# Convolution and attention on one core: vectors laid out by products, a first norm by blocks, and biases in another order

## The chip, the cores and the metric

The kernel runs on 1 core of a Trainium2 chip. Its time is device time in microseconds (us). The kernel before took 2860.66 us, the median of 6 runs (2857.87 to 2861.8). The profile is that of one more execution. Engines: PE multiplies matrices (and is fed by weight loads), DVE is the vector engine, ACT the scalar engine, POOL the general one, SP issues DMAs.

## The reference

For 4 images of 384 channels and 48x48 pixels (N = 2304 tokens) it computes a block of a network:

```python
local = lax.conv_general_dilated(x, conv_w, window_strides=(1, 1), padding='SAME', ..., feature_group_count=C)   # 7x7, each channel alone
inv = bn_gamma * lax.rsqrt(bn_var + BN_EPS)
local = local * inv[None, :, None, None] + (bn_beta - bn_mean * inv)[None, :, None, None]
x_norm = _layernorm(x_flat, ln_gamma, ln_beta)
qkv = x_norm @ qkv_w.T + qkv_b            # 8 heads of 48
q = q + _layernorm(local_flat, ln_gamma, ln_beta)   # by heads
attn = jax.nn.softmax(jnp.einsum('bhnd,bhmd->bhnm', q, k) * scale, axis=-1)
out = jnp.einsum('bhnm,bhmd->bhnd', attn, v)
return x_flat + (out @ proj_w.T + proj_b)
```

All is float32.

## The kernel before

**Tiles.** Channels lie on the 128 partitions in three chunks, in an order packed by heads (`segments`): each load of a group is four DMAs. Tokens come in groups of 384 (8 image rows), 6 groups to an image, 24 groups (`t`) in all. A group of three blocks of 128 tokens is the unit of the norms, of the queries and of the convolution; its convolution reads a slab of up to 14 rows (8 and 3 on each side).

**Norm.** The class `Norm` (L355 to L468) does a layer norm over channels: the mean by a product with a matrix of 1/384 on PE (`mean`, L386, or `mean_of`, through `project`, L473), centring on DVE (L401), squares on ACT (L364), the mean of the squares, Ln, Exp and a square on ACT (`root`, L406 to L408), two Newton steps on DVE (L413, L414) and the scaling (L468). Norms of later groups sum the three chunks on DVE (L374, L375) and send one product to PE.

**Convolution.** `conv_ops` (from L229) yields one DVE instruction for each chunk and tap: 147 of them (3 x 49) for a group (L251 the first tap, L255 the others). All 24 groups form one stream, and `convolve_first(n)` or `convolve(point)` take the next n of it. Chunk 0 of the first group is special: its first `PE_TAPS` = 10 taps are made on PE, as products with diagonal matrices (`make_diagonals` on ACT, L263; `first_products`, L274), and are added by `add_products` (L825). `AHEAD` = 4 of chunk 0's other taps come first.

**Order.** The order of work on PE, DVE, ACT, SP and POOL is that in which the code is written, engine by engine; every engine takes its instructions in order. A planner (`plan`) spreads what is left of the stream over the half-slots of the attention, so that a group's steps are done when its norm is due.

**Head.** Batch-norm and layer-norm vectors and the taps are combined into `natural` (L160 to L165) and moved by 14 small DMAs (L175, on ACT's and POOL's queues) into `vec`, packed by heads. x of the first group and the slab of the first convolution are loaded apart (`load_x`, `load_slab`, L106), then three weight tensors (`staged`), then x of the other groups, and `w_o`. 12 warm-up products (`warm`, L830) run on PE, then the mean of the first group, 12 more, and the rest of the first norm. ACT scales the weights by the norm's gain (L605 for values, L612 and L613 for keys and queries). The beta part of the biases is made by `shift_rows` (L568, one row each on PE), `rows_out` (L580, L583, ACT) and `columns` (L594, PE), and added by `key_bias` and `query_bias` (L616 to L622, DVE).

**Keys and values.** `from_x` makes values (by blocks), keys and queries of a group, two products of the list at a time; each call of `both(making)` goes on by one pair. For the first image this is done group by group (the loop over g from 1 to 5), interleaved with the norm of the next group's x and with convolution steps; in the last round the norm is that of the first convolution (`local_end`, L642), and `query_end` (L651) adds it to the queries.

**Attention.** For each group t come 12 slots of two halves, each of three blocks of keys: `score` (L765 on PE, Exp on ACT, L773) and `weigh` (L786 on PE). After each pair of heads ACT copies and DVE adds the sums (L672, L681). In slots 8 and 10 of the first group, 6 and 9 of the others, the norm of the next group's convolution is done: sums on DVE, from t = 1 on with two small DMAs (`out`, `few_in`), `few_centre` on DVE (L445), squares as `jobs` between the Exps on ACT (L369). In slot 3 of t = 0 `output_bias` folds the value bias into the output bias: 9 products of one column, a copy on ACT (L634), an addition on DVE (L635).

**End.** The last six groups are projected; between them `judge` counts reciprocals outside a safe range: a comparison on DVE (L1071), a product on PE (L1073), a decision (L1076, L1077), a read.

Of the kernel before, what the change touches and what calls it, by code (L numbers as in the profile page):

```python
# [15 lines left out]
P = 128  # L16
NH = 8
HD = 48
# [8 lines left out]
X_LATER = 3  # L27
OUT_SLOT = 4
LAG = 2
AHEAD = 4  # L30
WARM = 12
PE_TAPS = 10

# [11 lines left out]
def unshifted_pass(  # L47
# [49 lines left out]
    def two_banks():  # L97
        return next(either)()

    def over_chunks(a):  # L100
        return a.rearrange("p (o g) -> p o g", o=1).to_broadcast([P, CC, G])

    def load_packed(dst, src, queue=nc.sync, tails=None):
        for p0, piece in segments(src):
            by = tails if tails and p0 % 64 else queue
            by.dma_start(out=dst[p0 : p0 + piece.shape[0]], in_=piece)  # L106


    xn = {}

    def load_x(b, g):
        t = big.tile([P, CC, G], F32, tag=f"xn{g}", name=f"xn{b}_{g}")
        load_packed(t, x[b, :, g * G : (g + 1) * G])
        xn[b, g] = t

    slabs = {}

    def load_slab(b, g, tails=None):
        first, end = max(0, g * RG - PAD), min(H, (g + 1) * RG + PAD)
        t = work.tile([P, CC, (RG + 2 * PAD) * W], F32, tag="slab", name=f"slab{b}_{g}")  # L120
        load_packed(t[:, :, 0 : (end - first) * W], x[b, :, first * W : end * W], tails=tails)
        slabs[b, g] = (t, first, end)


# [28 lines left out]
    nc.scalar.dma_start(out=norms[:, 4:6], in_=ln)  # L153
    taps_in = big.tile([P, CC, T0], F32, tag="kt0", name="taps_in")
    nc.scalar.dma_start(out=taps_in, in_=conv_w)
    load_x(0, 0)
    load_slab(0, 0)
    nc.gpsimd.tensor_scalar_add(inv, norms[:, 3], BN_EPS)
    nc.gpsimd.tensor_tensor(inv, inv, neg_half, ALU.pow)
    nc.vector.tensor_copy(natural[:, :, T0 + 1 :], norms[:, 4:6].rearrange("p v c -> p c v"))  # L160
    nc.vector.tensor_mul(inv, inv, norms[:, 0])
    nc.vector.tensor_mul(natural[:, :, T0], norms[:, 2], inv)
    nc.vector.tensor_sub(natural[:, :, T0], norms[:, 1], natural[:, :, T0])
    for c in range(CC):
        nc.vector.tensor_scalar(  # L165
            natural[:, c, 0:T0], taps_in[:, c], inv[:, c : c + 1], None, ALU.mult
        )
    queues = cycle((nc.gpsimd, nc.scalar, nc.gpsimd))
    for c in range(CC):
        for r, n, first in ((0, HD, 0), (64, HD, 1), (48, 16, 6), (112, 16, 7)):  # L170
            head = first + 2 * c if first < 6 else first
            ch = head * HD + (16 * c if first >= 6 else 0)
            while n:
                part = min(n, P - ch % P)
                next(queues).dma_start(  # L175
                    out=vec[r : r + part, c, :],
                    in_=natural[ch % P : ch % P + part, ch // P, :],
                )
                r, n, ch = r + part, n - part, ch + part

# [47 lines left out]
    def conv_ops(t):  # L230
        b, g = divmod(t, NG)
        if t + 1 < NT:
            load_slab(*divmod(t + 1, NG))
        slab, first, end = slabs[b, g]
        acc = work.tile([P, CC, G], F32, tag="acc", name=f"acc{t}", bufs=3)
        accs[t] = acc
        if t == 0:
            nc.vector.memset(acc[:, 0, :], 0.0)

        order = [(tap, c) for tap in taps for c in range(CC)]  # L240
        if t == 0:
            mine = [(tap, 0) for tap in taps[PE_TAPS:]]
            order = mine[:AHEAD] + [o for o in order if o[1]] + mine[AHEAD:]
        for tap, c in order:
            part = window(slab, acc[:, c, :], g, first, end, c, tap)
            if not part:
                continue
            src, dst = part
            weight = cw[:, c, tap : tap + 1]
            if tap == taps[0]:  # L250
                nc.vector.tensor_scalar(  # L251
                    dst, src, weight, shift[:, c : c + 1], ALU.mult, ALU.add
                )
            else:
                nc.vector.scalar_tensor_tensor(dst, src, weight, dst, ALU.mult, ALU.add)  # L255
            yield
# [93 lines left out]
    class Norm:  # L350
# [9 lines left out]
            self.src = src  # L360
            self.buf = work.tile([P, CC, G], F32, tag="sq", name="sq")

        def squares(self):
            nc.scalar.activation(self.buf, self.src, AF.Square)  # L364

        def square_jobs(self):

# [13 lines left out]
            self.add(self.buf)  # L381


        def mean(self):
            self.m = two_banks()[:, 0, :G]
            nc.tensor.matmul(self.m, lhsT=mean_w, rhs=self.buf[:, 0, :], start=True, stop=True)  # L386

        def mean_kept(self):
# [3 lines left out]
            self.m = self.buf[:, 0, :]  # L392
            nc.scalar.copy(self.m, m)

        def mean_of(self, src):

            self.m = two_banks()[:, 0, :G]
            project(self.m, lambda c: mean_w, lambda c: src[:, c, :])

        def centre(self):  # L400
            nc.vector.tensor_sub(self.src, self.src, over_chunks(self.m))  # L401

        def root(self):

            y, u = self.buf[:, 1, :], self.buf[:, 2, :]
            nc.scalar.activation(u, self.m, AF.Ln, bias=eps)  # L406
            nc.scalar.activation(y, u, AF.Exp, scale=-0.5)
            nc.scalar.activation(u, y, AF.Square, scale=0.5**0.5)  # L408

        def newton(self):  # L410

            y, u = self.buf[:, 1, :], self.buf[:, 2, :]
            nc.vector.scalar_tensor_tensor(u, self.m, eps, u, ALU.add, ALU.mult)  # L413
            nc.vector.scalar_tensor_tensor(y, u, -1.5, y, ALU.add, ALU.mult)  # L414
            return over_chunks(y)

# [47 lines left out]
            nc.vector.transpose(self.buf[:, 2, :], spread(y))  # L464
            return over_chunks(self.buf[:, 2, :])

        def scale(self, rs):
            nc.vector.scalar_tensor_tensor(self.src, self.src, -1.0, rs, ALU.mult, ALU.mult)  # L468


    def project(dst, weights, src, n=G):
# [77 lines left out]
    def both(making):  # L549
        next(making)  # L550
        next(making)
# [36 lines left out]
    def columns():  # L588

        r, r2 = two_banks(), two_banks()  # L590
        m = {1: r[:, 0, 0:CC], 2: r[:, 1, 0:CC], 0: r2[:, 0, 0:CC]}
        for i in m:
            for c in range(CC):
                nc.tensor.matmul(  # L594
                    m[i][:, c : c + 1],
                    lhsT=row[of_row(i), c * P : (c + 1) * P],
                    rhs=one[of_row(i)],
                    start=True,
                    stop=True,
                )  # L600
        return m

    def scale_values():
        for c in range(CC):
# [225 lines left out]
            nc.tensor.matmul(first_sum[:, 0:P], lhsT=mean_w, rhs=ident, start=True, stop=True)  # L830

    warm(WARM)
    norm = Norm(xn[0, 0])
    norm.mean_of(norm.src)
    warm(WARM)
    norm.centre()
    norm.squares()
    make_diagonals(0, 5)
    convolve_first(AHEAD)
    norm.mean_of(norm.buf)  # L840
    norm.root()
    scale_values()
    first_products(5)
    norm.scale(norm.newton())
    make_diagonals(5, PE_TAPS)
    for c in range(CC):
        scale_rows(1, c)

# [1 line left out]
    both(making)  # L850
    shift_rows()
    rows_out()
    first_products(PE_TAPS - 5)
    m = columns()
    convolve_first(14)
    norm = Norm(xn[0, 1])
    norm.sum()
    norm.mean()
    add_products()
    key_bias(m)  # L860
    query_bias(m)
    both(making)
    convolve_first(3)
    norm.centre()
    norm.squares()
    convolve_first(4)
    norm.sum_squares()
    norm.mean()
    norm.root()
    for c in range(CC):  # L870
        scale_rows(0, c)
    both(making)
    convolve_first(10)
    norm.scale(norm.newton())
    both(making)
    both(making)
    for g in range(1, NG):

        last = g == NG - 1
        making = from_x(0, g)  # L880
        both(making)
        convolve_first(4)
        assert not last or n_first >= each - PE_TAPS
        norm = Norm(accs[0] if last else xn[0, g + 1])
        norm.sum()
        norm.mean()
        convolve_first(6)
        norm.centre()
        norm.squares()
        both(making)  # L890
        convolve_first(3)
        norm.sum_squares()
        norm.mean()
        norm.root()
        both(making)
        convolve_first(8 if last else 12)
        if last:
            local_end(0, norm.newton())
        else:
            norm.scale(norm.newton())  # L900
        both(making)
        both(making)
# [3 lines left out]
    for t in range(NT):  # L906
# [52 lines left out]
        for s in range(NSLOT):  # L959
# [31 lines left out]
            if t and following and s == second:  # L991
                norm.few_variance()
            convolve("slot", t, s, 0)
            if t == 0 and s == CC:
                output_bias()
            if t == 0 and s in (first, second):
                norm.mean_kept()
            attend(t, s, 1)
# [37 lines left out]
    for before in range(NT - NG, NT):  # L1036
        ao = aos[before % NG]
        if before == NT - NG + 3:
            judge[0](two_banks()[:, 0, :])
        r, r2 = two_banks(), two_banks()  # L1040
        parts = r[:, 0, :G], r[:, 1, :G], r2[:, 0, :G]
        for co, m in enumerate(parts):
# [2 lines left out]
            finish(before, co, m, nc.scalar)  # L1045
        if before == NT - NG:
            rb = divide(NT - 1)
        if before == NT - NG + 3:
            judge[1]()
        if before == NT - NG + 2:  # L1050
            nc.vector.tensor_mul(outputs[NT - 1][0], outputs[NT - 1][0], rb)
        if before == NT - 2:
            n_outside = judge[2]()
    return n_outside


def conv_attention(tc: tile.TileContext, *args):
    nc = tc.nc
    few = NH * RG * 48 // P
    with tc.tile_pool(name="keep", bufs=1) as keep:  # L1060
# [6 lines left out]
        nc.vector.memset(inside, 1.0)  # L1067
        nc.vector.memset(ones, 1.0)

        def count(m):  # L1070
            nc.vector.tensor_scalar(outside, inside, 0.5, None, ALU.is_lt)  # L1071
            counts.append(m[0:1, :few])
            nc.tensor.matmul(counts[0], lhsT=ones, rhs=outside, start=True, stop=True)  # L1073

# [4 lines left out]
        def read():  # L1079
            return nc.values_load(flag[0:1, 0:1])  # L1080

        n_outside = unshifted_pass(tc, *args, inside, (count, decide, read))
        with tc.If(n_outside > 0):
            shifted_pass(tc, *args)

# [504 lines left out]
```

## Time and profile before

| What | Value |
| --- | --- |
| median of 6 runs | 2860.66 us |
| the profiled execution: whole time | 2859.14 us |
| its span, first to last instruction | 2857.4 us |
| PE busy | 2833.8 us (99%) |
| DVE busy | 2341.7 us (82%) |
| ACT busy | 1648.1 us (58%) |
| POOL busy | 17.3 us (1%) |
| DMA moved | 124.38 MB, mean 44 GB/s |
| mean granted clock of PE | 0.999 |

Times in the text are microseconds from the start of this span. In a timeline a line has start, length, engine, line of the code, operation, tile written, tiles read, and in brackets the idle time before it and what ended it. A float32 product shows as two records. The list of waits has who waited, for whom, the sum, the number and the longest. The chain of waits goes back from the last instruction to what released it.

### The profile page before, as it was taken

How to read it: one execution, taken by the hardware profiler on the slowest of the kernel's cores; microseconds unless marked ns; L12 is line 12 of the kernel's file. 1: busy time of each engine (PE TensorE's matmuls, PEld its weight loads, DVE VectorE, ACT ScalarE, POOL GpSimd, SP SyncE). 2: the span in 40 equal slices, each digit the busy share in tenths (PEclk: the TensorE clock that was granted, in tenths of full speed). 3: DMA queues.
4: the chain of work that ended last, by engine and by line, in shares of the span. 5: the costliest groups of instructions: out<-in, count | busy, mean ns of one | idle time of the engine just before them, and what ended most of it. 6: DMA issues, size and time to landing. Idle time of an engine off the chain costs nothing.

```text
span 2857.4 us, 70279 instructions
## 1 busy us (share of the span) xinstructions
PE 2833.8 (99%) x29540; PEld 1453.8 (51%) x29540; DVE 2341.7 (82%) x4613; ACT 1648.1 (58%) x2341; POOL 17.3 (1%) x82
## 2 busy tenths in 40 slices
PE   8999999999999999999999999999999999999998
PEld 5544444444554455555555445555555545555554
DVE  7999999999888888888888889888788887787301
ACT  4366666666226666666623666666642466666662
POOL 2000000000000000000000000000000000000000
PEclk9999999999999999999999999999999999999999
DMA  6101121101221111111132112102113110111111
GB/s 116 39 11 31 46 48 35 38 25 42 74 80 30 40 35 42 30 39 24 38 95 69 27 30 51 35 22 45 38 32 94 45 22 28 43 30 30 45 34 63
DMA packets 103689, 124.38 MB, mean 44 GB/s; under 512 B 43344, under 2 KB 89024, under 8 KB 103360
## 3 DMA queue, kind: packets, MB, share of 16 engines
q1 hardware_dynamic: 99568, 116.07, 16.9%
q8 instruction: 234, 3.83, 0.6%
q10 hardware_dynamic: 3088, 3.65, 0.4%
q14 instruction: 95, 0.78, 0.1%
q0 software_dynamic: 704, 0.06, 0.0%
HBM read 81.98 MB, written 27.03 MB: 38 GB/s over the span
## 4 chain that ended last, share of the span: by engine, by line
PE 95%; DVE 3%; DMA 1%; ACT 0%; issue 0%; ACTq 0%; SPq 0%; DVEq 0%
PE r L765 38%; PE o L786 38%; PE o L473 10%; PE r L473 9%; DVE acc L255 2%; DMA xn<-in_x_dram 1%; ACT pt L773 0%; DMA vec<-natural 0%; PE r L386 0%; DMA staged<-in_qkv_wT_dram 0%; DMA taps_in<-in_conv_w_dram 0%; PE o L386 0%; DVE sq L375 0%; DMA parts<-part 0%; DVE sq L374 0%
## 5 line engine op out<-in xcount | busy, mean ns | idle before, releaser
L773 ACT ACTIVATE pt<-r 128x768 f32<-128x768 f32 x1728 | 1399.0, 810 | 757.4 <-PE r L765 741.2
L255 DVE SCALAR_TENSOR_TENSOR acc<-slab,vec,acc 128x368 f32<-128x368 f32 (+6 forms) x3447 | 1756.8, 584 | 3.7 <-DMA qk_vec<-in_qk_b_dram 2.6
L786 PE MATMUL o<-pt,v 64*64 64x384 f32 x13824 | 1438.9, 482 | 0.0
L765 PE MATMUL r<-xn,k 48*64 48x384 f32 x10368 | 1080.6, 482 | 4.7 <-ACT pt L773 4.7
L786 PEld LDWEIGHTS o<-pt,v 64*64 64x64 f32 x13824 | 552.3, 132 | 566.2 <-issue 562.6
L765 PEld LDWEIGHTS r<-xn,k 48*64 48x64 f32 x10368 | 414.5, 132 | 430.7 <-issue 394.5
L765 PE MATMUL r<-qt,kt 48*64 48x384 f32 x3456 | 359.4, 481 | 0.1
L765 PEld LDWEIGHTS r<-qt,kt 48*64 48x64 f32 x3456 | 136.9, 132 | 143.1 <-issue 133.7
L681 DVE TENSOR_TENSOR ao<-o,ao 113x384 f32<-113x384 f32 x72 | 40.0, 555 | 193.3 <-PE r L765 176.3
L473 PE MATMUL o<-xn,w_qk 128*128 128x384 f32 x432 | 147.2, 486 | 0.0
L473 PE MATMUL r<-xn,w_qk 128*128 128x384 f32 x432 | 147.2, 486 | 0.0
L473 PEld LDWEIGHTS r<-xn,w_qk 128*128 128x128 f32 x432 | 82.1, 190 | 57.2
L473 PEld LDWEIGHTS o<-xn,w_qk 128*128 128x128 f32 x432 | 82.0, 190 | 57.4 <-ACT w_qk L613 0.4
L506 ACT COPY v<-r 128x384 f32<-128x384 f32 x43 | 18.6, 482 | 135.2 <-PE r L473 135.2
L473 PE MATMUL r<-w_v,xn 128*128 128x384 f32 x258 | 87.3, 487 | 0.0
L681 DVE TENSOR_TENSOR aot<-o,aot 113x384 f32<-113x384 f32 x24 | 13.3, 556 | 82.1 <-ACT aot L672 64.5
L473 PE MATMUL o<-af,w_o 128*128 128x384 f32 x222 | 75.0, 486 | 0.0
L374 DVE TENSOR_TENSOR sq<-sq 128x384 f32<-128x384 f32 x47 | 26.1, 554 | 58.4 <-ACT sq L369 56.5
L473 PEld LDWEIGHTS r<-w_v,xn 128*128 128x128 f32 x258 | 48.8, 190 | 35.2 <-issue 1.8
L473 PE MATMUL o<-w_v,xn 128*128 128x384 f32 x174 | 60.3, 486 | 1.5 <-DVE xn L468 1.5
L741 DVE SCALAR_TENSOR_TENSOR xr<-r,pb,xr 128x384 f32<-128x384 f32 x27 | 16.4, 617 | 52.4 <-ACT xn L525 42.4
L473 PEld LDWEIGHTS o<-af,w_o 128*128 128x128 f32 x222 | 42.1, 190 | 29.2
(128 smaller groups left out, 1030.4 us busy)
## 6 DMA issues: line engine op xcount, KB each, us to landing
xr<-in_x_dram SPq DMA_DIRECT2D x24, 576.0 KB
slab<-in_x_dram SPq DMA_DIRECT2D x32, 378.0 KB
held<-ao SPq DMA_DIRECT2D x20, 576.0 KB
af<-held SPq DMA_DIRECT2D x20, 576.0 KB
xn<-in_x_dram SPq DMA_DIRECT2D x48, 216.0 KB
rb<-rden SPq DMA_DIRECT2D x48, 216.0 KB
out_dram<-xr SPq DMA_DIRECT2D x54, 192.0 KB
slab<-in_x_dram SPq DMA_DIRECT2D x16, 297.0 KB
```

Source lines behind the costliest of these rows:

```text
L255: nc.vector.scalar_tensor_tensor(dst, src, weight, dst, ALU.mult, ALU.add)
L374: nc.vector.tensor_add(self.buf[:, 0, :], src[:, 0, :], src[:, 1, :])
L473: nc.tensor.matmul(dst, lhsT=weights(c), rhs=src(c), start=c == 0, stop=c == CC - 1)
L506: nc.scalar.copy(v[:, blk, :, 0:HD], r[:, :C].rearrange("p (h d) -> p h d", d=HD))
L681: nc.vector.tensor_add(dst, sums[0 : 64 + HA, 1, :G], dst)
L741: nc.vector.scalar_tensor_tensor(xr[:, co, :], m, pb[:, co : co + 1], xr[:, co, :], ALU.add, ALU.add)
L765: nc.tensor.matmul(r[h, j, :G], lhsT=kk[:, blk * P + h.start : blk * P + h.stop], rhs=qq, start=True, stop=True,)
L773: nc.scalar.activation(pt, r[:, :, :G], AF.Exp, scale=SCALE)
L786: nc.tensor.matmul(sums[halves[j], i, :G], lhsT=values[t // NG, kb // NB][h, first : first + 64], rhs=pt[h, j, :], start=kb == 0, stop=kb ...
```

## The change

- **Vectors.** The 14 DMAs into `vec` go. DVE fills `packing` with columns of the identity (a memset, 14 copies), and `pack` moves `natural` into `vec` with 7 products on PE and one copy on ACT.
- **Loads.** The first group's x is no longer loaded; the first slab comes in two parts, its 8 rows and then 3 rows of the next group, and the first norm reads the slab.
- **First norm.** Means, centring, squares, roots, Newton steps and scaling go by three blocks of 128 tokens; the second warm-up goes. `scale_values` stands between the second and the third root.
- **Convolution.** `PE_TAPS` becomes 8, 2 of them early; `AHEAD` goes: chunks 1 and 2 of the first group come first.
- **Biases.** The remaining diagonals, the scaling of the query weights and six products come behind the first keys; the mean of the next x comes right behind the columns, in a bank of theirs; the second pair of keys comes ahead of that norm's second mean.
- **Output bias.** `output_bias` moves from slot 3 of the first attention into the last round of keys, between 4 convolution steps and the sums of the local norm.
- **Judge.** The comparison is a function of its own, behind the last division.

```diff
-PE_TAPS = 10
+PE_TAPS = 8
+EARLY_TAPS = 2
...
-    load_x(0, 0)
-    load_slab(0, 0)
+    load_slab(0, 0, parts=2)
+    place_x(0, 0)
...
+    packing = big.tile([P, len(pairs), P], F32, tag="k1", name="packing")
+    nc.vector.memset(packing, 0.0)
+    for c, r, cc, r0, n in pieces:
+        nc.vector.tensor_copy(
+            packing[:, pairs.index((c, cc)), r : r + n], ident[:, r0 : r0 + n]
+        )
...
-                next(queues).dma_start(
-                    out=vec[r : r + part, c, :],
-                    in_=natural[ch % P : ch % P + part, ch // P, :],
+    def pack():
+        m = two_banks()[:, 0, 0 : CC * (T0 + 3)].rearrange("p (c v) -> p c v", c=CC)
...
+                nc.tensor.matmul(
+                    m[:, c, :],
+                    lhsT=packing[:, pairs.index(pair), :],
+                    rhs=natural[:, pair[1], :],
...
+        nc.scalar.copy(vec, m)
...
             mine = [(tap, 0) for tap in taps[PE_TAPS:]]
-            order = mine[:AHEAD] + [o for o in order if o[1]] + mine[AHEAD:]
+            order = [o for o in order if o[1]] + mine
...
     warm(WARM)
+    pack()
+
+    blocks = [slice(i * P, (i + 1) * P) for i in range(NB)]
+    raw = slabs[0, 0][0]
     norm = Norm(xn[0, 0])
-    norm.mean_of(norm.src)
-    warm(WARM)
-    norm.centre()
-    norm.squares()
-    make_diagonals(0, 5)
-    convolve_first(AHEAD)
-    norm.mean_of(norm.buf)
-    norm.root()
+    norm.mean_of(raw, blocks)
+    for at in blocks:
+        norm.centre(raw, at)
+        norm.squares(at)
+    convolve_first(2)
+    norm.mean_of(norm.buf, blocks)
+    norm.root(blocks[0])
+    make_diagonals(0, EARLY_TAPS)
+    norm.root(blocks[1])
     scale_values()
-    first_products(5)
-    norm.scale(norm.newton())
-    make_diagonals(5, PE_TAPS)
+    norm.root(blocks[2])
+    first_products(EARLY_TAPS)
+    for at in blocks:
+        norm.scale(norm.newton(at), at)
+        if at is blocks[1]:
+            convolve_first(3)
     for c in range(CC):
         scale_rows(1, c)
...
     rows_out()
-    first_products(PE_TAPS - 5)
-    m = columns()
-    convolve_first(14)
+    make_diagonals(EARLY_TAPS, PE_TAPS)
+    next(making)
+    for c in range(CC):
+        scale_rows(0, c)
+    first_products(PE_TAPS - EARLY_TAPS)
+    m, bank = columns()
+    convolve_first(10)
     norm = Norm(xn[0, 1])
     norm.sum()
-    norm.mean()
-    add_products()
+    norm.mean(bank)
+    convolve_first(7)
     key_bias(m)
     query_bias(m)
-    both(making)
-    convolve_first(3)
+    next(making)
     norm.centre()
     norm.squares()
-    convolve_first(4)
+    both(making)
+    add_products()
+    convolve_first(2)
     norm.sum_squares()
     norm.mean()
     norm.root()
-    for c in range(CC):
-        scale_rows(0, c)
     both(making)
-    convolve_first(10)
+    convolve_first(6)
     norm.scale(norm.newton())
     both(making)
-    both(making)
+    convolve_first(5)
...
         assert not last or n_first >= each - PE_TAPS
+        if last:
+            output_bias()
...
-            if t == 0 and s == CC:
-                output_bias()
...
         if before == NT - NG:
             rb = divide(NT - 1)
+            judge[0]()
```

## The prediction

> **What bounds the kernel now.** I read the page first, then PE's waits, then the chain of waits between 212 and 312 us, then busy time by stretch, then the timeline of three places. The page says that PE hardly rests:
>
> ```profile
> span 2857.4 us, 70279 instructions
> ...
> PE 2833.8 (99%) x29540; PEld 1453.8 (51%) x29540; DVE 2341.7 (82%) x4613; ACT 1648.1 (58%) x2341; POOL 17.3 (1%) x82
> ```
>
> Only 23.6 us of PE's span are idle, 6.84 of them after its last matmul (2850.56). The list of PE's waits tells where the rest lies:
>
> ```profile
> PE r L765 <- ACT pt L773: 4.7, 5, 3.5
> PE o L386 <- DVE sq L375: 3.6, 2, 3.4
> PE r L1073 <- DVE outside L1071: 2.1, 1, 2.1
> ```
>
> The second is in the head (at 38.60), the third near the end (at 2832.74). The first names ACT, but the chain shows what ACT itself waited for:
>
> ```profile
> 306.21 1.37 DVE acc L445
> ...
> 308.03 0.80 ACT pt L773
> ...
> 308.88 0.88 PE r L765 x8
> ```
>
> ACT could not square (L369) before DVE had centred (L445), so PE stood still for 3.53 us until 308.88. DVE had been late for long. Busy time by stretch (length, then PE, PEld, DVE, ACT, POOL, then granted clock):
>
> ```profile
> 145.00:165.00 20.00, 19.71 (x239) 9.08 (x241) 20.00 (x40) 13.21 (x17) 0.00 (x0) 1.00 0.02 6
> 185.00:205.00 20.00, 20.00 (x252) 9.37 (x248) 20.00 (x40) 12.65 (x17) 0.00 (x0) 1.00 0.01 2
> ...
> 245.00:265.00 20.00, 20.00 (x252) 9.33 (x248) 20.00 (x40) 12.81 (x17) 0.00 (x0) 1.00 0.06 14
> ```
>
> From the end of the keys (143.18) to 306 DVE rests 0.79 and 0.43 us. So PE bounds the whole, but **until 308 it is DVE that sets when PE goes on**: what delays DVE before 306 delays the end, and what frees PE there is waited away.
>
> **The change, part by part** (times of the trace; the order and the waits are those of the two programs' instruction lists).
>
> *Vectors by products.* Fourteen DMAs of `vec` go. DVE gets a memset of 896 columns (0.8: L238 takes 0.38 for 384) and 14 copies, at 0.03 each (spacing of two memsets at 0.82) to 0.2 (dependent vector steps, L161 to L162): 0.4 to 2.8 us. Both end before the taps land at 5.46, and DVE waits for those anyway (L165), so they cost nothing; without that cover, up to 3.6. `natural` is full at 6.04, PE leaves its warm-up at 6.7. Seven products follow; none of that form is in the trace. Bounds: 0.09 each (0.223 of a 128-column warm-up matmul, scaled to 52 columns) and 0.43 (the same matmul at half clock); I take 0.223, the spacing of output_bias's one-column products: 1.56 us, to 8.3.
>
> *First norm by blocks.* Nine means at 0.223 end at 10.3 (before: 9.15). The first block's centring waits for the ninth mean, so DVE starts at 10.5 instead of 9.35; three steps of 0.5 (L374, 384 columns) and a square of 0.52 lead to 12.6, and the last block's means to 13.7 (root before: 14.28). A block's root is 0.40+0.35+0.31 (L406 to L408 less 256 columns at 0.83 ns, the slope between 384 and 1152 columns of square). ACT: root to 14.75, two diagonals at 0.295 (L263) to 15.35, root to 16.4, three `w_v` at 0.54 (L605) to 18.05, third block's Ln to 18.45. DVE's first Newton step waits for that Ln: **the blocks do not overlap where it matters.** Newton and scale take 1.3 a block; the first value matmul starts at 19.95, not 18.77.
>
> *Slab instead of x.* 576 KB fewer are loaded ahead of the weights; at the 172 GB/s of the first 40 us they land 3.4 us sooner. That is hidden: `w_v` (landed 16.85) is now wanted at 16.4, the last weights (23.7) at 23.9.
>
> *Biases in another order.* PE: two blocks of values 3.87 to 23.85, shift rows 2.26 to 26.1, value and key 3.87 to 30.0, six products (3.65, one more than the five at 26.01) to 33.6, columns 1.25, mean, result at 35.75; before, DVE centred at 32.31. Now it waits (its 17 steps are done at 34.0) and centres at 36.1; 1.35 + 0.6 + 1.0 + 1.15 end at 40.2 (before 38.46). The 3.38 us wait at 38.60 goes, since two keys now lie ahead of that mean. Root and six steps, Newton 1.2, scale 1.36: 45.9 as before, but five steps (2.6) still follow. Then 6.2 to the centring of group 1: 54.7 against 53.79, where DVE idled 1.95. **+0.9.** PE (two keys to 39.5, mean at 40.35, queries 5.8) is 2.3 early, 46.8 for 49.07, and waits for DVE. The rounds from there repeat every 19 to 20 us, so the distance stays.
>
> *Clock.* The granted clock fell once, after PE's stop at 308:
>
> ```profile
> 33.53:36.95 3.42, 1.69 (x6) 0.68 (x4) 2.07 (x5) 1.69 (x3) 0.00 (x0) 1.00 1.08 210
> 36.95:40.36 3.41, 1.76 (x6) 1.13 (x7) 3.02 (x6) 1.13 (x3) 0.00 (x0) 1.00 1.12 198
> ...
> 306.60:310.01 3.41, 1.13 (x16) 0.54 (x20) 3.41 (x6) 2.41 (x5) 0.00 (x0) 1.00 0.32 43
> 310.01:313.43 3.42, 3.42 (x28) 1.49 (x24) 3.32 (x8) 1.85 (x3) 0.00 (x0) 0.50 0.00 0
> ```
>
> A stretch with 1.13 us of matmul was followed by 3.41 us at half clock; stretches with 1.69 were not. The change drops the second warm-up and lets PE wait from 16.7 to 19.95: the stretch 16.47 to 19.88 on the same grid holds some 0.45 us of matmul. So I expect half clock to 23.3, 1.65 us of PE's work lost, and DVE's wait for the mean passes it on. Bounds 0 and 1.65; I take **+1.65**. The Trainium skill (TensorE: Matmul & The Clock Gate, Part 1: The HAM clock gate) lets the clock fall after a wholly idle window of about 3.4 us; by that rule it would hold here and the sum be 1.65 less, but the row above shows a fall with a third of the stretch busy.
>
> *Output bias with the last keys.* This is the largest term. Before:
>
> ```profile
> 126.29 4.03 PE L473 MATMUL o<-w_v,xn 128*128 128x384 f32 x12
> ...
> 126.66 0.55 DVE L374 TENSOR_TENSOR sq<-acc 128x384 f32<-128x384 f32 x1
> ...
> 131.00 1.35 DVE L401 TENSOR_TENSOR acc<-acc,r 128x1152 f32<-128x1152 f32 x1 [0.20 <-PE r L386]
> ```
> ```profile
> 172.15 2.17 PE L473 MATMUL r<-vbp,w_o 128*128 128x1 f32 x18
> ...
> 174.55 0.16 DVE L635 TENSOR_TENSOR pb<-pb,added 128x3 f32<-128x3 f32 x1 [0.79 <-ACT added L634]
> ```
>
> In the last group DVE is ready to sum at 126.66, while PE is in the values until 130.16. Now the addition to `pb` stands ahead of that sum. It waits for the values, then nine products (2.0) and ACT's copy (0.5): 132.6. Behind it on DVE are the sum (1.15) and six steps (3.0): centring at 136.8 instead of 131.0, **+5.8**, with the local norm, query_end and all of DVE's backlog behind it; PE waits for the sum and then for the squares. If PE were as far ahead as its values allow (at the scale's end, 124.83), the wait would still cost 4.4. At 172 the old place gives back 0.79 and 0.08 of DVE: **-0.87**; PE's 2.0 there only lengthen its wait for DVE.
>
> *Eight taps on PE.* Of the first 156 steps 139, not 137, belong to the first group; the plan makes up the other two by 306: 2 x 0.52 = **+1.04**.
>
> *Judge.* The comparison now stands at 2821.6, so PE's wait for L1071 goes; the next products have their operands and buffers: **-2.06**.
>
> Sum: 0.9 + 1.65 + 5.8 - 0.87 + 1.04 - 2.06 = +6.5. The profiled execution (span 2857.4, whole time 2859.14) would become 2865.6; the median lies 1.52 above it, so 2867.1, say 2867.
>
> **Rivals.**
> 1. *The clock holds.* For: a wait of 3.38 us at 35.2 left it alone. Then +4.8: 2865.5.
> 2. *DVE's wait in the last group is hidden* (not slower): it decides if DVE's steps before 306 have room I do not see, or DVE reaches group 5 more than 5.8 us behind PE. For: PE gains 2.3 us in the head. Against: at 115.89 PE waits 1.05 for DVE in group 4, and no idle DVE time follows. With the clock holding, 0.9 - 0.87 + 1.04 - 2.06 = -1.0: 2859.7.
> 3. *PE bounds alone*: DVE catches up, and PE keeps its lead of 2.3, loses the waits of 3.53 and 2.06 and the half clock (1.7): -9.6, 2851. For: PE's 99%. Against: DVE's full stretches from 143 on.
> 4. *The new small steps are dear*: products at 0.43 (+1.5), weights no sooner (+0.4), block steps at the cost of 384 columns (+1.5): some +9.9, 2870.5.
>
> **How the numbers follow.** Forecast 0.40, rival 1 0.24, rival 2 0.17, rival 3 0.09, rival 4 0.10. A measurement of this kernel tells about 0.2% (5.7 us) from no change. Forecast and rival 4 lie above: slower 0.50; rivals 1 and 2 within: 0.41; rival 3: faster 0.09. The range leaves out rival 3 and the dearest end of rival 4: 2858 to 2870.5.
>
> **What would show it.** First value matmul near 20, half clock around 20 to 23; group 1's values near 47 to 48.5; DVE idle some 6 us ahead of the `pb` addition near 135; PE's stop near 315 at least as long as 3.5 us; no wait at the count. Wrong if DVE's addition comes without a wait, or PE's stop near 308 shrinks.

## The result, and the profile after

The changed kernel takes 2866.0 us, the median of 20 runs (2864.99 to 2867.34); the kernel before took 2860.47 beside it (40 runs, 2857.37 to 2862.4). The ratio is 1.002, 95% interval 1.0014 to 1.0026: 5.5 us slower, just under the 5.7 us that were called telling. So by the prediction's own bar this is no change, to which it gave 0.41, less than the 0.50 for slower. The forecast was 2867.

The first lines of the changed kernel's page, and its shares of the chain of waits by engine:

```profile
span 2865.2 us, 70303 instructions
...
PE 2837.3 (99%) x29550; PEld 1869.6 (65%) x29550; DVE 2345.7 (82%) x4638; ACT 1651.6 (58%) x2348; POOL 12.8 (0%) x73
...
PE 92%; DVE 7%; DMA 0%; ACT 0%; issue 0%; SPq 0%; DVEq 0%; ACTq 0%
```

PE is as busy as before, and that says nothing: DVE's share of the chain has risen from 3% to 7%. PE's waits (for whom, sum, number, longest):

```profile
PE r L410 <- DVE sq L399: 6.4, 6, 1.9
PE r L794 <- ACT pt L802: 4.6, 5, 3.5
PE r L502 <- DVE xn L497: 2.8, 1, 2.8
PE r L415 <- DVE sq L399: 2.6, 2, 2.1
```

The wait for the comparison (L1071 before) is gone; three of the four groups are waits for DVE, and all of these lie before 320 us. The chain there (start, length, what) is the one of before, 8.75 us later:

```profile
314.96 1.37 DVE acc L473
...
316.79 0.80 ACT pt L802
...
317.63 1.56 PE r L794 x8
```

L473 is `few_centre`, 306.21 in the kernel before (L445 there). I call its start **the centring** below: it is where DVE hands its delay on to PE, by way of ACT's square (L393). Where the delay came from shows in the last group of the first image; timeline of the changed kernel, with the idle time before a line in brackets:

```profile
129.81 4.03 PE L502 MATMUL o<-w_v,xn 128*128 128x384 f32 x12
...
133.68 2.06 PE L502 MATMUL r<-vbp,w_o 128*128 128x1 f32 x18
...
135.97 0.16 DVE L664 TENSOR_TENSOR pb<-pb,added 128x3 f32<-128x3 f32 x1 [5.23 <-ACT added L663]
136.05 0.55 DVE L398 TENSOR_TENSOR sq<-acc 128x384 f32<-128x384 f32 x1
...
139.85 1.35 DVE L427 TENSOR_TENSOR acc<-acc,r 128x1152 f32<-128x1152 f32 x1
```

DVE stands still for 5.23 us in front of an addition of three columns. That centring, 131.00 before, is 8.85 us later, and the distance is nearly the same, 8.75 us, at the later one.

The clock, by stretches (length; busy time of PE, PEld, DVE, ACT, POOL; granted clock; DMA's share and GB/s). In each trace the clock changes only at edges that lie multiples of 3.41 us apart (in before 6.23, 310.01 and 313.43); I call these edges the grid. Where the grid lies differs from one execution to the next:

```profile
16.03:19.45 3.42, 0.76 (x3) 0.15 (x1) 1.16 (x4) 3.33 (x11) 0.00 (x0) 1.00 1.08 218
19.45:22.86 3.41, 3.23 (x5) 1.85 (x6) 3.27 (x10) 2.60 (x10) 0.00 (x0) 0.50 1.09 214
56.99:60.41 3.42, 1.51 (x5) 0.87 (x5) 3.39 (x9) 1.96 (x4) 0.00 (x0) 1.00 0.03 9
60.41:63.82 3.41, 3.41 (x7) 1.81 (x6) 3.41 (x8) 1.23 (x3) 0.00 (x0) 0.50 0.02 6
312.99:316.40 3.41, 1.15 (x16) 0.33 (x8) 3.34 (x7) 0.04 (x1) 0.00 (x0) 1.00 0.89 159
316.40:319.82 3.42, 2.19 (x16) 1.01 (x20) 3.42 (x8) 3.20 (x6) 0.00 (x0) 0.50 0.00 0
319.82:323.23 3.41, 3.41 (x26) 1.27 (x24) 3.24 (x8) 1.12 (x2) 0.00 (x0) 0.50 0.00 0
```

The fall at 19.45 was forecast. The one at 60.41, and the second half-clock stretch behind the stop, were not.

### The profile page after: what moved, and what is told of

The parts are those of the page before. It is cut to its first block, busy times and chain, and to the rows that moved or that the text cites. A ratio compares the mean times of both kernels' runs of the same rounds, so it can differ in the third digit from the quotient of the medians.

```text
span 2865.2 us, 70303 instructions
## 1 busy us (share of the span) xinstructions
PE 2837.3 (99%) x29550; PEld 1869.6 (65%) x29550; DVE 2345.7 (82%) x4638; ACT 1651.6 (58%) x2348; POOL 12.8 (0%) x73
## 4 chain that ended last, share of the span: by engine, by line
PE 92%; DVE 7%; DMA 0%; ACT 0%; issue 0%; SPq 0%; DVEq 0%; ACTq 0%
PE r L794 37%; PE o L815 37%; PE r L502 9%; PE o L502 9%; DVE acc L279 6%; DMA staged<-in_qkv_wT_dram 0%; DVE sq L399 0%; DVE sq L398 0%; DVE xn L427 0%; ACT pt L802 0%; DMA slab<-in_x_dram 0%; PE o L298 0%; DVE acc L275 0%; DVE xn L497 0%; DVE acc L427 0%
## 5 line engine op out<-in xcount | busy, mean ns | idle before, releaser
L279 DVE SCALAR_TENSOR_TENSOR acc<-slab,vec,acc 128x368 f32<-128x368 f32 (+7 forms) x3449 | 1758.2, 584 | 1.2
L815 PE MATMUL o<-pt,v 64*64 64x384 f32 x13824 | 1591.4, 483 | 0.0
L794 PE MATMUL r<-xn,k 48*64 48x384 f32 x10368 | 1189.9, 483 | 4.6 <-ACT pt L802 4.6
L815 PEld LDWEIGHTS o<-pt,v 64*64 64x64 f32 x13824 | 764.5, 133 | 359.5 <-issue 176.7
L794 PEld LDWEIGHTS r<-xn,k 48*64 48x64 f32 x10368 | 565.7, 133 | 283.7 <-issue 138.3
L794 PE MATMUL r<-qt,kt 48*64 48x384 f32 x3456 | 402.4, 482 | 0.1
L794 PEld LDWEIGHTS r<-qt,kt 48*64 48x64 f32 x3456 | 196.1, 133 | 85.0 <-issue 36.3
L502 PE MATMUL r<-w_v,xn 128*128 128x384 f32 x270 | 93.1, 494 | 2.8 <-DVE xn L497 2.8
```

The costliest lines, as they stand in the source:

```text
L502: nc.tensor.matmul(dst, lhsT=weights(c), rhs=src(c), start=c == 0, stop=c == CC - 1)
L794: nc.tensor.matmul(r[h, j, :G], lhsT=kk[:, blk * P + h.start : blk * P + h.stop], rhs=qq, start=True, stop=True,)
L815: nc.tensor.matmul(sums[halves[j], i, :G], lhsT=values[t // NG, kb // NB][h, first : first + 64], rhs=pt[h, j, :], start=kb == 0, stop=kb ...
```

## The experiments

**Theory.** Until the centring DVE sets when PE goes on, so the time goes by when DVE gets there: the output bias puts it off by some 4.9 us, the half clock of the head by most of the rest. **Rivals:** PE bounds all along and DVE's wait is hidden; the clock's falls lie beside other work; or the new head is what costs.

Both kernels and the twelve experiments, with the centring and the end of PE's last matmul in their profiled execution, and the difference of these two. Behind a median stands, in brackets, that of the kernel before, measured beside it.

| Kernel | median (before) | ratio, 95% interval | centring | last matmul ends | difference |
| --- | --- | --- | --- | --- | --- |
| before | | | 306.21 | 2850.56 | 2544.4 |
| changed | 2866.0 (2860.47) | 1.0014 to 1.0026 | 314.96 | 2859.96 | 2545.0 |
| b_judge | 2857.74 (2859.89) | 0.9983 to 1.0001 | 307.32 | 2849.24 | 2541.9 |
| b_bias | 2862.34 (2859.89) | 1.0 to 1.0018 | 312.27 | 2856.65 | 2544.4 |
| a_old_bias | 2860.99 (2859.89) | 0.9994 to 1.0012 | 310.18 | 2853.72 | 2543.5 |
| a_late_add | 2862.57 (2859.89) | 1.0 to 1.0018 | 310.75 | 2855.85 | 2545.1 |
| a_root | 2862.93 (2860.44) | 1.0 to 1.0018 | 311.53 | 2855.47 | 2543.9 |
| a_warm | 2863.6 (2860.44) | 1.0004 to 1.0022 | 311.85 | 2856.97 | 2545.1 |
| a_fill | 2862.15 (2860.44) | 0.9999 to 1.0017 | 311.74 | 2855.56 | 2543.8 |
| a_best | 2856.23 (2860.44) | 0.9978 to 0.9996 | 304.88 | 2848.14 | 2543.3 |
| a_taps10 | 2865.82 (2859.9) | 1.0013 to 1.0033 | 314.20 | 2857.57 | 2543.4 |
| b_plus | 2854.28 (2859.9) | 0.9971 to 0.9989 | 305.49 | 2847.53 | 2542.0 |
| b_thrice | 2863.76 (2859.9) | 1.0005 to 1.0024 | 312.28 | 2856.47 | 2544.2 |
| b_plus_warm | 2852.58 (2859.79) | 0.9966 to 0.9985 | 303.14 | 2845.34 | 2542.2 |

The centring ranges over 11.8 us, the difference over 3.2, and that falls into steps. Old end of the program: 2544.2 to 2544.4. With the early comparison: 2541.9 to 2542.2, 2.2 to 2.3 less. The changed kernel and its variants have the early comparison too, and stand 1.3 to 3.2 above b_judge: 1.4 is a drift told of below; 2545.0 or more where the clock stayed at half for two stretches behind PE's stop (changed, a_late_add, a_warm), 2543.9 for one (a_root), 2543.3 to 2543.8 for none. **When DVE reaches the centring is the time, but for the clock, the comparison and the drift.**

One fall of the clock behind the stop hardly shows in the difference (2544.4 with it in before, 2544.2 without it in b_thrice), because DVE is not done at 308. In b_judge, which has no fall there, ACT waits for the centrings of the next three groups too (1.33 us until 402.44, 1.32 until 496.21, 0.70 until 589.35; in before 0, 0.32 and 0.29), and matched product by product PE, which was spared the half clock, loses 1.4 us between 390 and 600 us instead.

### b_judge: the early comparison alone

```diff
-            judge[0](two_banks()[:, 0, :])
+            judge[1](two_banks()[:, 0, :])
...
             rb = divide(NT - 1)
+            judge[0]()
...
```

> The kernel before with one part of the change, the early comparison. Theory: PE's wait of 2.06 us for the comparison goes and nothing takes its place: the time falls by about 2.1 us, to 2858.4, and after the trace's last matmul the same 6.8 us follow. Rival: what ends the program is the last division, its transfers and the stores, not PE; then PE ends 2.1 us sooner, the idle stretch behind its last matmul grows by 2.1 us, and the time stays 2860.5.

Measured: 2.15 us less by the medians; the interval just reaches no change. Matched product by product, PE is 2.14 us further on behind the count than ahead of it, and 6.7 us follow its last matmul, as the 6.8 in before. The rival is out. This trace also shows a fall of the clock in the *old* head, which the profiled execution of before does not have:

```profile
36.29:39.70 3.41, 1.03 (x3) 0.68 (x4) 2.29 (x5) 1.16 (x2) 0.00 (x0) 1.00 1.13 195
39.70:43.11 3.41, 3.41 (x7) 1.88 (x6) 3.41 (x8) 3.35 (x11) 0.00 (x0) 0.50 1.06 168
...
172.82:176.23 3.41, 3.41 (x38) 2.53 (x34) 2.62 (x6) 1.39 (x4) 0.00 (x0) 1.00 0.01 2
176.23:179.65 3.42, 3.42 (x28) 1.46 (x24) 3.42 (x8) 0.81 (x1) 0.00 (x0) 0.50 0.02 6
...
307.66:311.07 3.41, 1.64 (x24) 0.52 (x16) 3.41 (x6) 2.36 (x5) 0.00 (x0) 1.00 0.18 27
```

From group 4 on, where I compared, DVE is 1.66 us later than in before, up to its last steps ahead of the centring (1.11 there). b_bias (38.47), b_thrice (38.32) and b_plus (37.99) fall there too; before was the only profiled execution of this head as it was that did not. And at 176.23 the clock falls behind a stretch that is full of matmuls; b_thrice was made for that.

### b_bias: the output bias in the last group, alone

```diff
         assert not last or n_first >= each - PE_TAPS
+        if last:
+            output_bias()
...
-            if t == 0 and s == CC:
-                output_bias()
```

> The kernel before with one part of the change, the output bias in the last group of the first image. Theory: DVE, ready for its sum at 126.7 us, waits some 6 us for PE's values, the nine products and ACT's copy; its centring in that group moves from 131.0 to about 136.8, every later step of DVE with it, and the old place gives 0.87 us back: +4.9 us, about 2865.4, with the stop of PE near 308 about 5 us later. Rival: the wait is hidden, since PE is the engine that is 99% busy: then DVE's late start is made up by 308 and the time stays within 1 us of 2860.5.

DVE waits 5.7 us in front of `pb`, and the centring is 4.95 us later than in b_judge, which has the same fall in the head: the 4.9 that were expected. The clock fell here too, from 134.05 to 140.87, but not ahead of the delay: DVE's sum, at 134.14, is 5.82 us later than in b_judge, and the last group's centring behind it 5.53. The median rose by only 2.45 us (interval 0 to 5.1), half of what was expected. In the profiled executions the last matmul is 6.1 us later than in before; b_judge is 0.8 later ahead of its count as well, and 1.9 us are given back behind the last matmul (4.9 us to the end of the span, for 6.8). Why that end is shorter is not shown; it takes from 4.9 to 6.8 us in the fourteen profiled executions. So the delay of DVE is shown; what it costs in the median is not well fixed.

### a_old_bias and a_late_add: the bias taken back, whole or in part

```diff
-        if last:
-            output_bias()
...
             convolve("slot", t, s, 0)
+            if t == 0 and s == CC:
+                output_bias()
```

> The changed kernel with the output bias back in its old place, the first attention tile. Theory: the 5.23 us that DVE stood still in the last group go and 0.87 us of waiting and adding come back: about 4.4 us less, 2861.6. Rival: the late start of DVE in the earlier groups (3.07 us after the second fall of the clock) or PE itself sets the end then, and under 1 us is gained: 2865 to 2866.

5.0 us less than the changed kernel, or 4.4 with each set against the kernel before beside it; the centring is 4.78 earlier. DVE's lines in the last group now follow one another with no idle time:

```profile
130.67 0.56 DVE L398 TENSOR_TENSOR sq<-acc 128x384 f32<-128x384 f32 x1
131.26 0.56 DVE L399 TENSOR_TENSOR sq<-sq,acc 128x384 f32<-128x384 f32 x1
...
134.47 1.34 DVE L427 TENSOR_TENSOR acc<-acc,r 128x1152 f32<-128x1152 f32 x1
```

```diff
         nc.scalar.copy(added, m)
-        nc.vector.tensor_add(pb, pb, added)
+        return added
...
         if last:
-            output_bias()
+            added = output_bias()
...
             convolve("slot", t, s, 0)
+            if t == 0 and s == CC:
+                nc.vector.tensor_add(pb, pb, added)
```

> The changed kernel with the nine products and ACT's copy of the output bias left in the last group, and only DVE's addition put off to the first attention tile. Theory: what costs is DVE standing at the head of its own list, not PE's work: the 5.23 us go, the addition costs its 0.1 us later and waits for nothing, so about 5.1 us less, 2860.9, some 0.8 us better than the old place of the whole. Rival: PE's 2.06 us of products put off the mean that DVE centres with; then it is some 2 us worse than the old place of the whole, 2863 or more.

Here my theory was too simple: 2862.57, 1.6 us worse than the old place and not 0.8 better. DVE's line and PE's two lines in the last group of a_late_add:

```profile
135.93 1.35 DVE L427 TENSOR_TENSOR acc<-acc,r 128x1152 f32<-128x1152 f32 x1 [1.88 <-PE r L410]
```
```profile
133.07 2.06 PE L502 MATMUL r<-vbp,w_o 128*128 128x1 f32 x18
135.00 0.89 PE L410 MATMUL r<-sq,mean_w 128*128 128x384 f32 x2
```

The nine products stand ahead of the mean that DVE's centring waits for, 1.88 us. At the later centring a_late_add is only 0.57 us behind a_old_bias, in an execution that was 0.5 us ahead when the last group began; a further 1.6 us come behind it, where the clock stayed at half for two stretches here and did not fall there. So the 4.8 us have two parts: an addition at the head of DVE's list, and products at the head of PE's. Both have to move.

### a_root, a_warm, a_fill: the head

```diff
-    scale_values()
     norm.root(blocks[2])
+    scale_values()
```

> The changed kernel with the third block's root ahead of the three scalings of w_v on ACT. Theory: DVE's first Newton step stood still for 5.44 us until the third block's Ln had run behind the scalings (17.84 us); now that Ln starts near 16.3, Newton near 16.7, and the first value product waits for the last scaling of w_v instead, near 18.9 for 19.63. Everything that DVE does until 308 us comes 0.7 us sooner: 2865.3. Rival: the blocks then overlap in full and the head gains the whole 1.5 us: 2864.5. Other rival: the columns of the biases or the weights set the head's pace, and nothing is gained.

Newton starts at 16.32 where it waited until 18.22 in the changed kernel, and 3.1 us are gained instead of 0.7. The first value product comes at 17.73 (19.63): it needs one scaled chunk of `w_v`, not the last one as I had it, so the rival's whole 1.5 us were there. The rest of the gain is clock: the stretch ahead of the old fall now holds 2.09 us and the fall is gone (the one near 60 us stays).

```diff
     first_products(EARLY_TAPS)
+    warm(12)
...
         norm.sum_squares()
+        if g == 1:
+            warm(6)
         norm.mean()
```

> The changed kernel with more warm-up products of 128 columns, into a bank that nothing reads, in two gaps of PE: 12 (2.7 us) behind the first two products of the convolution, and 6 (1.3 us) ahead of the second mean of group 1. Theory: the granted clock falls where a stretch of 3.41 us holds little of matmuls, so both falls of the head (19.45 and 60.41 us, each 1.7 us of PE's work) go, and since DVE waits for PE there, about 3 us go with them: 2863. The fall behind 316 us stays. Rival: PE's half clock in the head lies beside DVE's or ACT's work; then the falls go from the records but under 1 us from the time.

Both falls are gone from the records, PE is 3.1 us earlier from group 4 to 312, and the median fell by 2.4: as expected. One more thing follows. At the values of group 4 PE stood 3.07 us behind the profiled before; without the two falls it stands 0.03 us ahead of where before stood. **Without the falls of the clock the new head costs about nothing and gains nothing.**

```diff
     norm.mean(bank)
-    convolve_first(7)
+    convolve_first(13)
```

> The changed kernel with 13 steps of the convolution, not 7, ahead of the key bias in the first group. Theory: DVE stands still for 3.17 us there (until 36.14) and until 308 us it sets when PE goes on, so six steps of 0.52 us done in that gap are six steps fewer that it has to make up by then: 3.1 us less, 2862.9. Rival: the addition of the key bias comes later than its columns by the last of the six steps, the first centring and all that follows is late by it, and at most 1 us is gained.

The centring came 3.22 us sooner, and the median fell by 3.85 us. PE's own place in the last group barely moved (0.04 us at 150 us): steps done in a gap pay only where the backlog ends.

### a_taps10: ten taps on PE

```diff
-PE_TAPS = 8
+PE_TAPS = 10
```

> The changed kernel with ten taps on PE instead of eight, the one term of the sum that is left. Theory: two steps of 0.52 us go from what DVE has to do by 308 us, so its centring there, at 314.96 in the changed kernel, comes 1.0 us sooner, and the time is about 2865. Rival: the two products more (1.3 us) and ACT's two diagonals (0.6 us) put off the columns of the biases, for which DVE stood still 3.17 us; then DVE loses 1.3 to 1.9 in the head for the 1.0 it gains, and the time is 2866 to 2867.

Undecided by time: 0.2 us less than the changed kernel, 0.4 more when each is set against the kernel before beside it. The centring came 0.76 sooner for the 1.04 of the prediction, and in the head DVE waited 5.8 us for the columns (3.17 without the edit), in an execution whose clock stayed at half from 18.40 to 25.23. Both sides of the trade are there, and they nearly cancel.

### a_best, b_plus, b_plus_warm: what the reasons are good for

a_best has a_root's, a_warm's and a_fill's edits, `PE_TAPS = 12`, a_late_add's addition in slot 3 of t = 0, and the products here in the last round:

```diff
         norm.mean()
         norm.root()
+        if last:
+            added = output_bias()
```

> All of the mends together: the third block's root ahead of the scalings, both sets of warm-up products, 13 steps in DVE's gap, 12 taps on PE instead of 8, the nine products of the output bias behind the second mean of the last group and its addition in the first attention tile. Theory: 0.7 for the root, 3 for the clock, 3.1 for the gap, 2.1 for four steps less on DVE and 5.2 for the output bias make 14 us of DVE's delay at 308 us; PE's own stop there (3.5 us and the clock's 3.4 behind it) is all that it can give beyond the 4.4 us by which PE follows, so PE bounds the rest: 2855. Rival: DVE stays the later one past 308 us, since 16 products more on PE (the taps' four and the warm-up) delay its columns: 2859 or more.

2856.23, faster than both kernels. The centring came 10.1 us sooner, not 14: the savings overlap. b_plus goes back to the old head, with the early comparison, the output bias moved in the same way, and more steps in a gap of DVE:

```diff
-        convolve_first(6)
+        convolve_first(10 if g == 1 else 6)
         norm.centre()
```

> The kernel before with the old head, the early comparison, the products of the output bias behind the second mean of the last group and its addition in the first attention tile, and four more steps of the convolution in DVE's gap of 1.95 us in group 1. Theory: DVE's centring near 306 comes 0.8 us sooner for the bias and up to 2 for the gap; PE's stop of 3.53 us shrinks by as much, to about 1, and with it the fall of the clock behind it (1.7 us of PE's work) goes from most executions; the comparison gives its 2.1: 2855 to 2856, as good as the changed kernel with all mends, without the new head. Rival: the new head is what the mended kernel lives on; then this one stays at the 2858 of the early comparison alone.

2854.28, a little below its forecast: 5.6 us under the kernel before beside it, where a_best is 4.2 under; the intervals overlap. The new head is not needed. But the fall in the old head was there again, so I took it away:

```diff
     norm.sum_squares()
-    norm.mean()
+    spare_banks = two_banks()
+    for _ in range(12):
+        nc.tensor.matmul(spare_banks[:, 1, 0:P], lhsT=mean_w, rhs=ident, start=True, stop=True)
+    norm.m = spare_banks[:, 0, :G]
+    nc.tensor.matmul(norm.m, lhsT=mean_w, rhs=norm.buf[:, 0, :], start=True, stop=True)
     norm.root()
```

> The kernel of the run before (the old head, the early comparison, the output bias behind the second mean, four steps more in DVE's gap) with 12 warm-up products of 128 columns ahead of the second mean of group 1, where PE waits 3.38 us for DVE's sum of squares. Theory: the stretch that holds this wait has 0.03 us of matmul, and the fall behind it (37.99 to 41.41) costs 1.7 us that DVE hands on to its centring at 305.5; with 2.7 us of products in the gap no stretch of the head holds under 1.6 us, the fall goes, the centring comes near 303.9, PE's stop there shrinks from 1.9 us to under 0.5, and the time falls by 1.5 to 1.7 us: 2852.7. Rival: PE's half clock lies beside DVE's steps in this kernel, or PE bounds it by now; then it stays within 0.5 us of 2854.3.

The stretch of the gap in b_plus, and the two that cover it in b_plus_warm:

```profile
34.58:37.99 3.41, 0.03 (x2) 0.05 (x1) 1.67 (x4) 2.01 (x3) 0.00 (x0) 1.00 1.09 225
37.99:41.41 3.42, 3.42 (x6) 1.91 (x7) 3.42 (x8) 1.74 (x4) 0.00 (x0) 0.50 1.02 194
```
```profile
33.22:36.63 3.41, 3.27 (x26) 2.84 (x24) 1.67 (x5) 2.02 (x3) 0.00 (x0) 1.00 1.05 225
36.63:40.04 3.41, 2.85 (x9) 1.82 (x10) 3.41 (x8) 1.86 (x5) 0.00 (x0) 1.00 1.07 193
```

2852.58, ratio 0.9975 (0.9966 to 0.9985): the best of all, 7.2 us under the kernel before. The time was the expected one; PE's stop was not. It stayed at 2.0 us, since PE came 2.4 us sooner as well, and the clock fell behind it.

### b_thrice: what the clock counts

```diff
+        for _ in range(3):
             for co in range(CC):
                 project(m[:, co : co + 1], ...)
```

> The kernel before with the output bias's 18 one-column matmuls run three times over in the old place (54 of them, some 6.5 us for 2.17; the result is that of the last round). Theory: such products fill PE's time in the records but count as idle to the clock, so a whole stretch of 3.41 us of nothing else comes about in any execution, and the granted clock falls to 0.5 in the stretch behind it, near 176 to 180 us. PE is 4.3 us and some 1.7 to 2.5 later for it, of which its stop of 3.53 us near 308 takes up what it can: 2863, and no stop there. Rival: what the clock goes by is PE's busy time; then there is no fall near 176, PE's 4.3 us less 3.5 cost under 1 us, and the fall behind the stop at 308 goes: 2859 to 2861.

```profile
174.86:178.27 3.41, 3.41 (x33) 3.41 (x32) 0.29 (x1) 0.00 (x0) 0.00 (x0) 1.00 0.02 5
178.27:181.69 3.42, 3.42 (x22) 3.01 (x25) 0.50 (x2) 0.16 (x1) 0.00 (x0) 0.50 0.00 0
181.69:185.10 3.41, 3.41 (x28) 1.35 (x24) 3.41 (x8) 0.81 (x1) 0.00 (x0) 0.50 0.00 1
```

The first of these stretches, in which PE did one-column products from end to end, was followed by half clock. So was the next, which ends them and has only 0.79 us of other products. As to the time, 2863.76 was right for a wrong reason: DVE's addition waited 6.0 us for the longer products (0.79 in before), and the stop near 308 did not vanish (1.4 us). It is the delay of DVE again.

## Why the prediction was right, and where it was not

**DVE sets the pace until 308:** right, by the table of centrings. The signs that it named came: the first value product at 19.63, half clock from 19.45 to 22.86, group 1's values at 48.15, DVE idle for 5.23 us ahead of `pb`, a stop of 3.5 us until 317.63 and no wait at the count. Rivals 2 (hidden) and 3 (PE bounds alone) are out: b_bias and a_old_bias move the centring by 4.95 and 4.78 us, and the end with it. "Until 308" is too early an end, since DVE holds PE at the next three centrings too where the clock does not.

**Output bias, +5.8 and -0.87, net 4.93:** at the centring 4.95 in b_bias, 4.78 in the changed kernel; by the medians 2.45 and 4.4. Right in place, and in size at the centring, but the price belongs to two instructions' places, on DVE and on PE; the working named only DVE's.

**Head, +0.9:** about 0, by a_warm. The step about the blocks ("do not overlap where it matters") was right: Newton waited 5.44 us, until 18.22.

```profile
18.22 0.35 DVE L441 SCALAR_TENSOR_TENSOR sq<-o,eps,sq 128x128 f32<-128x128 f32 x1 [5.44 <-ACT sq L434]
```

**Half clock, +1.65:** the fall at 19.45 came where it was put (forecast 19.88), but there were two falls in the head, 3.1 us together by a_warm. What failed is the reading "a wait of 3.38 us at 35.2 left it alone". It did so in that execution only, because the edge of two stretches cut the wait into halves (1.69 and 1.76 us of matmuls). The Trainium skill (TensorE: Matmul & The Clock Gate, Part 1: The HAM clock gate) says that the window by which the clock is set runs freely and doesn't reset when a kernel starts. The traces agree: the first rise to full clock lies anywhere from 4.75 to 8.01 us in the profiled executions, and the same gap fell or held by it. The clock fell there in four of the five profiled executions of the old head as it was, so before probably pays for it in most of its runs, and its profiled execution was a quick one, 1.3 us under the median. (b_judge's profiled execution, with the fall, took 2857.74; with the comparison's 2.14 added that is 2859.88, and the median of before beside it is 2859.89.)

That section's rule that an idle window lowers the clock, read as a wholly idle one, is contradicted as in the prediction, now by more rows: stretches with up to 1.57 us of wide matmuls (128 columns or more) were followed by a fall, those with 1.62 or more were not. Between 1.54 and 1.57 both happened (a fall behind 14.83 in a_old_bias and 216.62 in a_root, none behind 142.05 in a_fill and 59.36 in a_taps10), so there busy time alone does not decide.

**Eight taps, +1.04:** 0.76 in a_taps10 at the centring, paid back in the head: nothing by the time. **Judge, -2.06:** -2.14.

**By the medians:** 4.4 (a_old_bias), 2.4 (a_warm) and -2.15 (b_judge) make 4.65 of the 5.5, each with an interval of some us.

**Not in the sum:** a second half-clock stretch behind the stop, some +1.4 (the extra half of a stretch less what PE would have waited); the drift, +1.4; a wait of DVE on a DMA near 305 that is gone, -0.43; a shorter end behind the last matmul (5.2 us for 6.8), -1.6, its cause not shown. From profile to profile that makes +8.75 at the centring, +1.35, +1.4, -2.1 and -1.6, the 7.8 us between the two spans. The medians are 5.5 apart, since before's profiled execution lay below its median and the changed kernel's 1.0 above. So 2866.0 lies between the forecast (2867) and rival 1 (2865.5), and only the trace tells the two apart: the clock did not hold. That the number came so near owes something to errors that cancel: the second fall (+1.5), the longer one behind the stop and the drift against the head (-0.9), the DMA (-0.4), the end (-1.6) and a base, before's profiled execution, that was itself a quick one.

**Left open.** The drift: matched product by product, the profiled executions of the changed kernel and its seven variants lose 1.4 us between 900 and 2800 us against before (10.10 to 11.52 us in the changed kernel), in instructions that are the same; the five kernels made from before lose nothing. Weight loads are busy for 63 to 66% of the span in the former, for 50 to 53% in the latter and in before. Which of the changes brings it was not tried. Also open: why the end behind the last matmul differs.

## What to carry to other kernels

Find the instruction at which a late engine hands its delay to the bounding one, and judge every edit ahead of it by what it does to that start; a three-column addition in front of a full list, with the products that feed it, put that start off by 4.8 us, more than anything else in this change. Put small cross-engine sums where all their inputs are long done, on each engine that they pass, not on one. A profiled execution is one draw of the clock's grid: before pricing a gap by whether the clock fell, ask what the same gap does when the grid lies 1.7 us elsewhere.

## What the hardware showed that I had not expected

One-column products (18 in 2.06 to 2.17 us, 0.12 a record) fill PE's time in the records and still let the clock fall: at 176.23 behind a stretch of 3.41 us busy of 3.41 in b_judge, at 178.27 in b_thrice, and at 134.69 in a_root and 137.87 in a_taps10, where the stretches had 1.81 us busy, 0.86 and 0.11 of it in wide products. A stretch of the changed kernel with the same 1.81 us busy, 1.57 of it wide (135.50 to 138.91), was followed by full clock. So the clock does not go by the busy time of the records. A fall lasts more than one stretch when the next one is not filled: behind a fall, stretches at half clock with 0.97 to 2.68 us of wide matmuls (and b_thrice's, 3.42 us busy with 0.79 wide) were followed by another at half, those with 2.81 or more by full clock.
